# Attention and mixture block on one core: six of eight head groups go through Wo by seven products of halved operands

## The chip, the core and the metric

The kernel runs on one core of a Trainium2 chip. TensorE (PE) multiplies matrices and writes to PSUM; VectorE (DVE), ScalarE (ACT) and GpSimd (POOL) work on tiles of 128 partitions; SyncE (SP) issues all transfers between the chip's memory (HBM) and the tiles in SBUF. The metric is device time in microseconds (us), shown as the median of several runs. Before the change it is 1365.17 us (three runs, 1364.51 to 1367.77).

## The reference

Two batch rows b of 512 tokens with 512 features, all in float32. What matters of the computation:

```python
x  = hidden                                     # (2, 512, 512)
a  = layernorm(x)
q, k, v = a @ Wq + bq, a @ Wk + bk, a @ Wv + bv # inner width 32 heads * 128
q, k = rms_norm(q, gq), rms_norm(k, gk)
p  = softmax(q @ k.T / sqrt(128))               # for each head and batch row
o  = p @ v                                      # (2, 512, 32 * 128)
x  = x + layernorm(o @ Wo + bo)                 # Wo is 4096 x 512
x  = x + layernorm(ffn(layernorm(x)))           # a base product and 8 gated experts of rank 16
```

The change concerns `o @ Wo + bo`.

## The kernel before

The program is one list of instructions whose order on PE, DVE, ACT and POOL is the order in which the code is written (`manual_schedule`, with these four in `IN_ORDER`). Only the place of SP's transfers among each other is left to the scheduler. An instruction that waits holds up all that stand behind it on its engine.

The work comes in stages. First x is loaded and normalized. Then `project` makes Q and afterwards K, group by group of four heads (`GH` = 4, eight groups), each group with seven products of halved operands (tokens of the two batch rows, halves of the features, halves of the group's columns) instead of eight. The finished heads go out to HBM (`keptq`, `keptk`). During Q's groups `value_sums` loads quarters of Wv, forms sums on POOL and stores them (`keptw`). During K's groups the q tiles are fetched back, scaled on DVE and stored (`keptqs`). V is made by `values`, a generator whose every step is one product tile of 512 columns on PE (two matmuls) and an exit from PSUM; finished V tiles go to HBM (`keptv`).

The head loop (`for i in range(N)`, lines 533 to 557) has 64 iterations, `i = 2 * head + batch row`. In iteration i the engines get, in this order: `sums(i - 1)` and `below_top(i)` on DVE (L459 and L467, L484), `scores(i + 1)` on PE with its four exits on ACT (L440, L441), the exponential of i on ACT (L487), `reciprocals` and `divided` for i - 1 (PE L473 writes psd, DVE L475, L477, L502, ACT L503), V steps if any are due, one tile of `outward`, `top_of(i + 1)` (DVE L450, L451, POOL L453), the exits of V and outward on DVE, and last `weighted(i)` on PE (L496), which needs the exponential of i. So PE's order within an iteration is scores, psd, V, outward, weighted. The first 28 V steps run ahead of the loop; 28 more are spread over i = 0 to 7 and the last 56 over i = 8 to 43 (the line that computes `want`).

`outward(g, n)` (L514) multiplies the four heads of group g, 128 tokens of one batch row, by four blocks of Wo into one PSUM tile, and adds it to one of eight tiles `ys` (L515). Group g is done during the eight iterations of group g + 1; the last group comes behind the loop.

A float32 matmul of 512 columns shows in the trace as two records, each with its own load of weights (PEld). PSUM tiles come from two tags, `ps` and `aux`, of four banks each; V, outward and weighted share `aux`. A pool has a fixed number of tiles, and a new one waits until one is free: `opool` holds finished heads, `hpool` the weights of V (three tiles of 512 KB), `wpool` the weights of Q and K and then Wo by groups (two of 1 MB), `vpool` the sums of weights and then V tiles, `kpool` and `qpool` the k and q tiles of the loop. `fetch(i + 3)` and `fetch_v` issue the loop's loads.

Of the kernel before, what the change touches and what calls it, by code (L numbers as in the profile page):

```python
# [10 lines left out]
F32 = mybir.dt.float32  # L11
AF = mybir.ActivationFunctionType
ALU = mybir.AluOpType
AX = mybir.AxisListType

P = 128
S = 512
D = 512
H = 32
INNER = H * P  # L20
NT = S // P
NK = D // P
GH = 4
E, R = 8, 16
# [7 lines left out]
def kernel(ctx: ExitStack, tc: tile.TileContext, x, wq, wk, wv, wo, vecs, rows, wbase, gates, bexp, out):  # L32
# [7 lines left out]

    nc = tc.nc
    B = x.shape[0]
    N = H * B

    const = ctx.enter_context(tc.tile_pool(name="const", bufs=1))
    xpool = ctx.enter_context(tc.tile_pool(name="xpool", bufs=B * NT))
    npool = ctx.enter_context(tc.tile_pool(name="npool", bufs=B * NK))
    ypool = ctx.enter_context(tc.tile_pool(name="ypool", bufs=B * NT))  # L50
    upool = ctx.enter_context(tc.tile_pool(name="upool", bufs=7))
    vpool = ctx.enter_context(tc.tile_pool(name="vpool", bufs=3 * NT))
    qpool = ctx.enter_context(tc.tile_pool(name="qpool", bufs=5))
    kpool = ctx.enter_context(tc.tile_pool(name="kpool", bufs=5))
    opool = ctx.enter_context(tc.tile_pool(name="opool", bufs=GH * B + 5))
    spool = ctx.enter_context(tc.tile_pool(name="spool", bufs=3))
    tmp = ctx.enter_context(tc.tile_pool(name="tmp", bufs=4))
    wpool = ctx.enter_context(tc.tile_pool(name="wpool", bufs=2))
    hpool = ctx.enter_context(tc.tile_pool(name="hpool", bufs=3))
    small = ctx.enter_context(tc.tile_pool(name="small", bufs=4))  # L60
    psum = ctx.enter_context(tc.tile_pool(name="psum", bufs=4, space=bass.MemoryType.PSUM))
    dram = ctx.enter_context(tc.tile_pool(name="dram", bufs=1, space=bass.MemoryType.DRAM))
# [12 lines left out]
            turn_of[0] += 1  # L75
        return psum.tile([P, 512], F32, tag=tag, name=name)

    def load_x(b, t, name):
        xt = xpool.tile([P, D], F32, tag="x", name=f"{name}{b}_{t}")
        nc.sync.dma_start(out=xt, in_=x[b, ts(t, P), :])  # L80
        return xt

    def load_w(src, name):

# [1 line left out]
        nc.sync.dma_start(out=w, in_=src.rearrange("(c p) f -> p c f", p=P))  # L86
        return w

    xs = [[load_x(b, t, "x") for t in range(NT)] for b in range(B)]
    wq0 = load_w(wq[:, ts(0, GH * P)], "w_q0")  # L90

    ident = const.tile([P, P], F32, tag="ident", name="ident")
# [57 lines left out]
    def token_sums(xTs):  # L150

        (b11, b21), (b12, b22) = ((xT[0:2], xT[2:4]) for xT in xTs)
        t1, t2, t3, t4 = (
            [xpool.tile([P, 512], F32, tag="x", name=f"t{i + 1}_{c}") for c in range(2)] for i in range(4)
        )
        for c in range(2):
            nc.vector.tensor_tensor(t1[c], b12[c], b11[c], ALU.subtract)
            nc.vector.tensor_tensor(t2[c], b22[c], t1[c], ALU.subtract)  # L158
            nc.vector.tensor_tensor(t3[c], b22[c], b12[c], ALU.subtract)
            nc.vector.tensor_tensor(t4[c], b21[c], t2[c], ALU.subtract)  # L160
        return [t1, t2, t3, t4]

    def weight_sums(w, name):

        a11, a12, a21, a22 = w[:, 0:2, 0:256], w[:, 2:4, 0:256], w[:, 0:2, 256:512], w[:, 2:4, 256:512]
        out = [vpool.tile([P, 2, 256], F32, tag="v", name=f"s{i + 1}_{name}") for i in range(4)]
        s1, s2, s3, s4 = out
        nc.gpsimd.tensor_tensor(s1, a21, a22, ALU.add)
        nc.gpsimd.tensor_tensor(s2, s1, a11, ALU.subtract)
        nc.gpsimd.tensor_tensor(s3, a11, a21, ALU.subtract)  # L170
        nc.gpsimd.tensor_tensor(s4, a12, s2, ALU.subtract)
        return [a11, a12, a22] + out
# [88 lines left out]
    def attention():  # L261
# [13 lines left out]
        G = GH * B  # L275
# [11 lines left out]
        def value_sums(p, c):  # L287
# [10 lines left out]
            for i, w in enumerate((s1, s2, s3, s4)):  # L298
                nc.sync.dma_start(out=keptw[p, i, c], in_=w)

        keptqs = dram.tile([B, H, P, 512], F32, tag="qs", name="keptqs")

        scale_steps = []
# [28 lines left out]
        for g in project(xTs, sums4, wq, bq, steps[:, 0, :], "q", [(qpool, "q")], keptq, accq, weight_sums(wq0, "q0")):  # L332
            if g == NG - 2:
                k_parts = weight_sums(load_w(wk[:, ts(0, GH * P)], "w_k0"), "k0")
            value_sums(g // 2, g % 2)
        for g in project(xTs, sums4, wk, bk, steps[:, 1, :], "k", [(kpool, "k"), (upool, "u")], keptk, acck, k_parts, between=scale_some):
            if g == 0:
                for b in range(B):
                    ssq = pt(f"ssq{b}")
                    nc.tensor.matmul(ssq, ones, accq[b], start=True, stop=True)  # L340
                    nc.scalar.activation(rqs[b], ssq, AF.Sqrt, bias=epst[:, 1:2], scale=1.0 / INNER)
                    nc.vector.reciprocal(rqs[b], rqs[b])
                scale_steps.extend(scalings())
# [8 lines left out]
        vs, wos = {}, {}  # L352

        def load_wo(g):
            wos[g] = load_w(wo[ts(g, GH * P), :], f"wo{g}")

        keptv = dram.tile([B, H // GH, NT, P, 512], F32, tag="v", name="keptv")

# [54 lines left out]

                    yield exits

        def fetch_v(b, g):
            for t in range(NT):
                v = vpool.tile([P, 512], F32, tag="v", name=f"v{b}_{g}_{t}")
                nc.sync.dma_start(out=v, in_=keptv[b, g, t])
                vs[b, g, t] = v  # L420

        qs, kk = {}, {}

# [62 lines left out]
        def exponentials(i):  # L486
            nc.scalar.activation(ss[i], ss[i], AF.Exp)  # L487

        os = {}

        def weighted(i):
            h, b = divmod(i, B)
            g, j = divmod(h, GH)
            po = pt(f"o{b}_{h}", "aux")
            for k in range(NT):
                nc.tensor.matmul(po, vs[b, g, k][:, ts(j, P)], ss[i][:, k, :], start=(k == 0), stop=(k == NT - 1))  # L496
            return po

        def divided(i, po, r):
            h, b = divmod(i, B)  # L500
            o = opool.tile([P, 512], F32, tag="o", name=f"oh{b}_{h}")
            nc.vector.tensor_tensor(o, po, r, ALU.mult)  # L502
            nc.scalar.activation(o, o, AF.Identity, bias=bv[:, h : h + 1], scale=1.0)  # L503
            os[b, h] = o

        ys = [ypool.tile([P, 512], F32, tag="y", name=f"y{n}") for n in range(B * NT)]

        def outward(g, n, tag=None):

            b, t = divmod(n, NT)  # L510
            ps = pt(f"psy{b}_{g}_{t}", tag or "aux")
            for j in range(GH):
                o = os[b, g * GH + j]
                nc.tensor.matmul(ps, o[:, ts(t, P)], wos[g][:, j, :], start=(j == 0), stop=(j == GH - 1))  # L514
            return lambda: nc.vector.tensor_tensor(ys[n], ps, bo_b if g == 0 else ys[n], ALU.add)  # L515


        v_steps = values()
        for n in range(28):
# [6 lines left out]
            if n == 18:  # L526
                scores(0)
                top_of(0)
        for b in range(B):
            fetch_v(b, 0)  # L530
        left = 28 * (NG // 2 - 1)
        po = None
        for i in range(N):
            g, n = divmod(i, G)
            if i + 3 < N:
                fetch(i + 3)
            if n == 2:
                load_wo(g)
            if n >= G - 2 and g + 1 < NG:
                fetch_v(n - G + 2, g + 1)  # L540
            part = sums(i - 1) if i > 0 else None
            below_top(i)
            if i + 1 < N:
                scores(i + 1)
            exponentials(i)
            if i > 0:
                divided(i - 1, po, reciprocals(i - 1, part))
            exits = []
            want = 28 * (i + 1) // G if i < G else 28 + 56 * (i + 1 - G) // (5 * G - 4)
            while left and 84 - left < want:  # L550
                exits.append(next(v_steps))
                left -= 1
            adds = [outward(g - 1, n)] if g > 0 else []
            top_of(i + 1)
            for work in exits + adds:
                work()
            po = weighted(i)
        divided(N - 1, po, reciprocals(N - 1, sums(N - 1)))
        again = [[kpool.tile([P, 512], F32, tag="k", name=f"xr{b}_{t}") for t in range(NT)] for b in range(B)]
        for b in range(B):  # L560
            for t in range(NT):
                nc.sync.dma_start(out=again[b][t], in_=x[b, ts(t, P), :])
        wb = load_w(wbase, "wb")
        bexp_sb = hpool.tile([P, 2, 512], F32, tag="h", name="bexp_sb")[:, 0, :]
        gate_sb = hpool.tile([P, 1024], F32, tag="h", name="gate_sb")[:, 0 : NK * (E * R + E + 1)].rearrange(
            "p (c f) -> p c f", c=NK
        )
        nc.sync.dma_start(out=gate_sb, in_=gates.rearrange("(c p) f -> p c f", p=P))
        nc.sync.dma_start(out=bexp_sb, in_=bexp)
        adds = [outward(NG - 1, n, "ps") for n in range(NT)]  # L570
        for add in adds:
            add()
        adds = [outward(NG - 1, NT + n, "aux") for n in range(NT)]
        for b in range(B):
            x2 = ys[b * NT : (b + 1) * NT]
            for _ in residual(again[b], x2, f"r{b}"):
                pass
            if b == 0:
# [31 lines left out]
    def ffn(b, xs, w, gate_sb, bexp_sb):  # L610
# [63 lines left out]
        zs = []  # L674
        for t in range(NT):
            nc.tensor.matmul(pss[t], hT[:, ts(t, P)], bexp_sb, start=False, stop=True)  # L676
            z = vpool.tile([P, 512], F32, tag="v", name=f"z{b}_{t}")
            nc.vector.tensor_tensor(z, pss[t], bbase_b, ALU.add)
            zs.append(z)
        yield  # L680
# [41 lines left out]
```

## Time and profile before

| | |
|---|---|
| median of three runs | 1365.17 us |
| the profiled execution | 1363.96 us, of which the span is 1362.2 |
| instructions | 10840 |
| Q stage, about 20 to 225 us | TensorE without idle time from 68 us on |
| K stage, about 225 to 418 us | DMA 312 to 337 GB/s from 272 us on |
| first V steps, 418 to 459 us, then the head loop to about 1265 us | TensorE full but for 3.26 us |
| last group through Wo, norms, mixture, 1265 to 1362 us | TensorE partly idle |
| scores, weighted and Wo on TensorE | 230.2, 230.3 and 230.8 us |
| V on TensorE | 208.3 us |
| traffic | HBM read 136.42 MB, written 77.59 MB |

How to read the profile: all times are in us from the span's start unless marked ns. Busy time counts an engine's instructions, not its waits. A row of the groups gives line, engine, operation, output and inputs, shape and count, then busy time in all and the mean of one in ns, then the engine's idle time ahead of these instructions and what ended it. A row of the timeline gives start, duration and the same names, and in brackets the wait ahead of it. The chain follows back from the last instruction what released each step. Rows of windows give each engine's busy time within a stretch, the granted TensorE clock, the DMA engines' busy share and GB/s. The span of matmuls overlaps with the next one's, so the distance between starts is what one costs in a stream.

### The profile page before, as it was taken

What the parts mean: (1) busy time and instruction counts of PE and PEld (TensorE: products, weight loads), DVE (VectorE), ACT (ScalarE), POOL (GpSimd) and SP (SyncE); (2) the same over time, 40 slices, a digit from 0 to 9 for tenths busy, and PEclk for the clock granted to TensorE, in tenths of its full rate; (3) what the DMA queues carried; (4) which work ended last, traced back from release to release, by engine and by line L of the source; (5) the groups of instructions that cost most, each with busy time, mean ns of one, the idle gap of its engine ahead of it and who ended that gap; (6) DMA issues with size and microseconds to landing.
All of it is one profiled execution on the core that took longest, in us unless ns stands there. A gap on an engine that the chain in (4) does not pass through costs nothing.

```text
span 1362.2 us, 10840 instructions
## 1 busy us (share of the span) xinstructions
PE 1319.9 (97%) x3244; PEld 599.4 (44%) x3244; DVE 926.2 (68%) x1206; ACT 488.0 (36%) x655; POOL 400.9 (29%) x294
## 2 busy tenths in 40 slices
PE   4999999999999999999999999999999999999976
PEld 2444444444444444444444444444444444444443
DVE  6443434777754478877777777777677888888566
ACT  4123232222131153443434334343433455444333
POOL 3478888565763011111111111111111111111000
PEclk9999999999998999999999999999999999999988
DMA  6486665599999865532343252352343131300101
GB/s 218 170 282 220 219 221 201 178 314 337 320 323 311 262 208 161 177 132 85 123 155 103 91 188 62 99 171 91 108 147 101 62 123 55 116 31 24 55 0 62
DMA packets 115083, 214.75 MB, mean 158 GB/s; under 512 B 10192, under 2 KB 10832, under 8 KB 115024
## 3 DMA queue, kind: packets, MB, share of 16 engines
q1 hardware_dynamic: 115024, 214.05, 47.0%
q8 instruction: 26, 0.43, 0.1%
q14 instruction: 33, 0.27, 0.1%
HBM read 136.42 MB, written 77.59 MB: 157 GB/s over the span
## 4 chain that ended last, share of the span: by engine, by line
PE 68%; DVE 2%; DMA 1%; ACT 0%; issue 0%; ACTq 0%
PE pss L440 16%; PE o L496 16%; PE psy L514 16%; PE v L384 14%; PE f L626 2%; PE p_k L192 2%; PE f L676 1%; PE psd L473 1%; PE hg L618 1%; DMA w_v<-keptw 1%; PE nt_f L139 0%; DVE st_z L123 0%; DVE quarters L459 0%; DVE s L484 0%; DVE z L600 0%; ACT s L487 0%
## 5 line engine op out<-in xcount | busy, mean ns | idle before, releaser
L441 ACT ACTIVATE s<-pss,rk 128x512 f32<-128x512 f32 x256 | 175.9, 687 | 464.6 <-PE pss L440 457.8
L453 POOL PARTITION_ALL_REDUCE top<-m x64 | 114.1, 1783 | 717.1 <-DVE m L451 717.1
L514 PE MATMUL psy<-wo,oh 128*128 128x512 f32 x512 | 230.8, 596 | 0.0
L496 PE MATMUL o<-s,v 128*128 128x512 f32 x512 | 230.3, 592 | 0.3 <-ACT s L487 0.3
L440 PE MATMUL pss<-qh,kh 128*128 128x512 f32 x512 | 230.2, 592 | 0.0
L496 PEld LDWEIGHTS o<-s,v 128*128 128x128 f32 x512 | 97.2, 190 | 123.1 <-issue 121.5
L440 PEld LDWEIGHTS pss<-qh,kh 128*128 128x128 f32 x512 | 97.3, 190 | 122.5 <-issue 122.5
L459 DVE TRANSPOSE_TENSOR_REDUCE quarters<-s 128x64 f32<-128x2048 f32 x64 | 147.3, 2301 | 0.0
L484 DVE TENSOR_TENSOR s<-s,top 128x2048 f32<-128x2048 f32 x64 | 146.0, 2281 | 0.0
L514 PEld LDWEIGHTS psy<-wo,oh 128*128 128x128 f32 x512 | 95.7, 190 | 112.4 <-issue 111.9
L487 ACT ACTIVATE s<-s 128x2048 f32<-128x2048 f32 x64 | 121.7, 1901 | 6.1 <-DVE s L484 6.1
L384 PE MATMUL v<-w_v,t 128*128 128x512 f32 x256 | 120.0, 613 | 3.3 <-DMA w_v<-keptw 3.3
L213 POOL TENSOR_TENSOR accq<-accq,sq_q 128x512 f32<-128x512 f32 x62 | 78.6, 1268 | 55.6 <-ACT sq_q L212 54.5
L213 POOL TENSOR_TENSOR acck<-acck,sq_k 128x512 f32<-128x512 f32 x62 | 85.4, 1382 | 24.7 <-ACT sq_k L212 21.7
L192 PE MATMUL p_q<-t,s_q 128*128 128x512 f32 x192 | 87.8, 607 | 2.6 <-DVE t L158 2.6
L384 PE MATMUL v<-w_v,nT_a 128*128 128x512 f32 x192 | 88.3, 601 | 0.0
L212 ACT ACTIVATE sq_k<-k 128x512 f32<-128x512 f32 x62 | 38.7, 630 | 137.8 <-DVE k L244 67.8
L212 ACT ACTIVATE sq_q<-q 128x512 f32<-128x512 f32 x62 | 39.1, 631 | 133.8 <-DVE q L244 78.2
L192 PE MATMUL p_k<-t,s_k 128*128 128x512 f32 x192 | 85.0, 592 | 0.0
L475 DVE RECIPROCAL inv<-psd 128x16 f32<-128x16 f32 x64 | 16.5, 257 | 99.6 <-PE psd L473 99.6
L450 DVE TENSOR_TENSOR m<-s 128x1024 f32<-128x1024 f32 x64 | 77.8, 1216 | 4.7 <-ACT s L441 4.7
L515 DVE TENSOR_TENSOR y<-psy,y 128x512 f32<-128x512 f32 x56 | 38.4, 691 | 57.6 <-PE psy L514 57.6
(152 smaller groups left out, 1418.5 us busy)
## 6 DMA issues: line engine op xcount, KB each, us to landing
keptq<-q SPq DMA_DIRECT2D x64, 256.0 KB, 4.0
q<-keptq SPq DMA_DIRECT2D x16, 1024.0 KB, 6.5
w_v<-keptw SPq DMA_DIRECT2D x32, 512.0 KB, 4.0
keptk<-k SPq DMA_DIRECT2D x64, 256.0 KB, 6.9
keptqs<-q SPq DMA_DIRECT2D x64, 256.0 KB, 6.9
qh<-keptqs SPq DMA_DIRECT2D x64, 256.0 KB, 2.9
kh<-keptk SPq DMA_DIRECT2D x64, 256.0 KB, 2.7
keptv<-o_v SPq DMA_DIRECT2D x64, 256.0 KB, 3.4
```

What stands on the lines that cost most here:

```text
L192: nc.tensor.matmul(ps, a[:, c, ts(j, P)], x[c], start=(c == 0), stop=(c == 1))
L212: nc.scalar.activation(sq, o, AF.Square)
L213: nc.gpsimd.tensor_tensor(accs[b], accs[b], sq, ALU.add)
L384: nc.tensor.matmul(ps, x[c][:, ts(t, P)], w[:, c, :], start=(c == 0), stop=(c == 1))
L440: nc.tensor.matmul(ps, kk[i][:, ts(k, P)], qs[i], start=True, stop=True)
L441: nc.scalar.activation(s[:, k, :], ps, AF.Copy, scale=rks[b][:, k : k + 1])
L453: nc.gpsimd.partition_all_reduce(ms[i], m[:, 0, :], P, ReduceOp.max)
L459: nc.vector.tensor_reduce(quarters.rearrange("p k j -> p (k j)"), ss[i].rearrange("p k (j r) -> p (k j) r", r=32), AX.X, ALU.add, apply_tr ...
L484: nc.vector.tensor_tensor(s, s, top.unsqueeze(1).to_broadcast([P, NT, 512]), ALU.subtract)
L487: nc.scalar.activation(ss[i], ss[i], AF.Exp)
L496: nc.tensor.matmul(po, vs[b, g, k][:, ts(j, P)], ss[i][:, k, :], start=(k == 0), stop=(k == NT - 1))
L514: nc.tensor.matmul(ps, o[:, ts(t, P)], wos[g][:, j, :], start=(j == 0), stop=(j == GH - 1))
```

## The change

For the first six of eight groups (`WG`), o @ Wo is computed by seven products in place of eight. The left operand is halved by batch row and by head within a pair of heads (2c and 2c + 1): a11, a12 are the pair's heads of row 0, a21, a22 those of row 1. The right operand is halved by head within the pair (k) and by columns of Wo (e, 256 each). Two pairs of a group are summed in PSUM.

- During Q's groups Wo's halves are loaded for these six groups (512 KB each, two for each group), four sums are formed in place on DVE (`output_sums`), and stored to HBM (`keptwo`).
- `head_sums(c)`, four DVE operations in every fourth iteration, forms the left sums of a pair.
- `through_wo(g, i, u)` is one task: product i, half u of the tokens, four logical matmuls of 256 columns into one PSUM tile. A group has 14 tasks, laid over the eight iterations of the next group. `load_right` fetches the right operand in rows of 1 KB, into two tiles of a new pool.
- The result is added to one of 14 running sums in SBUF, `acc[i][u]`; for the first group it is written by ACT, or by DVE together with a bias (products 1 and 5). Eight of the 14 lie in the two tiles of `wpool`, where Wo lay before.
- During the last group's iterations `combined` makes the eight y tiles from the running sums, 14 DVE operations, three an iteration. There group 6 goes through Wo as before, with each addition one iteration later; group 7 follows behind the loop as before. Their Wo blocks are now loaded in two halves, from `hpool`.
- V is fetched by pairs of heads, 512 KB in rows of 1 KB, one pair ahead, into four tiles; before it was fetched by groups in four transfers of 256 KB.
- Pools are reshaped to make room (x, weight sums and running sums in larger tiles, `opool` 16 instead of 13, z from `opool`, gates and expert weights from the new pool).

```diff
-    xpool = ctx.enter_context(tc.tile_pool(name="xpool", bufs=B * NT))
+    xpool = ctx.enter_context(tc.tile_pool(name="xpool", bufs=B * NT // 2))
-    ypool = ctx.enter_context(tc.tile_pool(name="ypool", bufs=B * NT))
+    ypool = ctx.enter_context(tc.tile_pool(name="ypool", bufs=6))
-    vpool = ctx.enter_context(tc.tile_pool(name="vpool", bufs=3 * NT))
+    vpool = ctx.enter_context(tc.tile_pool(name="vpool", bufs=4))
-    opool = ctx.enter_context(tc.tile_pool(name="opool", bufs=GH * B + 5))
+    opool = ctx.enter_context(tc.tile_pool(name="opool", bufs=16))
+    gpool = ctx.enter_context(tc.tile_pool(name="gpool", bufs=2))
...
+        def load_halves(g):
+            pool, tag = ((hpool, "h"), (gpool, "g"))[g % 2]
+            wo_halves[g] = [pool.tile([P, 2, 512], F32, tag=tag, name=f"wo{g}_{k}") for k in range(2)]
+            for k in range(2):
+                nc.sync.dma_start(out=wo_halves[g][k], in_=woq[g, k])
+        def output_sums(g):
+            of = wo_halves[g]
+            (b11, b12), (b21, b22) = ([w[:, :, ts(e, 256)] for e in range(2)] for w in of)
+            nc.vector.tensor_tensor(b11, b12, b11, ALU.subtract)
+            nc.vector.tensor_tensor(b12, b22, b12, ALU.subtract)
+            nc.vector.tensor_tensor(b22, b22, b11, ALU.subtract)
+            nc.vector.tensor_tensor(b21, b22, b21, ALU.subtract)
+            for k in range(2):
+                nc.sync.dma_start(out=keptwo[g, k], in_=of[k])
...
             value_sums(g // 2, g % 2)
+            if 0 < g <= WG:
+                output_sums(g - 1)
+            if g < WG:
+                load_halves(g)
...
-        def fetch_v(b, g):
-            for t in range(NT):
-                v = vpool.tile([P, 512], F32, tag="v", name=f"v{b}_{g}_{t}")
-                nc.sync.dma_start(out=v, in_=keptv[b, g, t])
-                vs[b, g, t] = v
+        def fetch_v(b, c):
+            v = vpool.tile([P, NT, 256], F32, tag="v", name=f"v{b}_{c}")
+            src = keptv[b, c // 2].rearrange("t p f -> p t f")
+            nc.sync.dma_start(out=v, in_=src[:, :, ts(c % 2, 256)])
+            vs[b, c] = v
...
+        def head_sums(c):
...
+            a11, a12, a21, a22 = (os[b, 2 * c + k] for b in range(B) for k in range(2))
+            s3, s2, s4 = tile_of(3), tile_of(2), tile_of(4)
+            nc.vector.tensor_tensor(s3, a11, a21, ALU.subtract)
+            nc.vector.tensor_tensor(a21, a21, a22, ALU.add)
+            nc.vector.tensor_tensor(s2, a21, a11, ALU.subtract)
+            nc.vector.tensor_tensor(s4, a12, s2, ALU.subtract)
+            left_of.update({(3, c): s4, (5, c): a21, (6, c): s2, (7, c): s3})
+        product_order = (1, 2, 4, 5, 7, 6, 3)
...
+        def through_wo(g, i, u):
+            ps = pt(f"psw{i}_{g}_{u}", "aux").rearrange("p (t e) -> p t e", t=2)
+            for t in range(2):
+                for j in range(2):
+                    a = left_of[i, 2 * g + j][:, ts(2 * u + t, P)]
+                    nc.tensor.matmul(ps[:, t, :], a, right_of[i, g][:, j, :], start=(j == 0), stop=(j == 1))
+            to = acc[i][u]
+            def add():
+                if g > 0:
+                    nc.vector.tensor_tensor(to, ps, to, ALU.add)
+                elif i in bias_of:
+                    nc.vector.tensor_tensor(to, ps, bias_of[i].unsqueeze(1).to_broadcast([P, 2, 256]), ALU.add)
+                else:
+                    nc.scalar.copy(to, ps)
+            return add
...
+        wo_tasks = {i: [] for i in range(N)}
+        for g in range(WG):
+            for k in range(14):
+                wo_tasks[G * (g + 1) + k * G // 14].append(
+                    lambda g=g, k=k: through_wo(g, product_order[k // 2], k % 2)
+                )
...
-            if n == 2:
-                load_wo(g)
-            if n >= G - 2 and g + 1 < NG:
-                fetch_v(n - G + 2, g + 1)
+            c, n4 = divmod(i, 2 * B)
+            if 2 <= n4 and 0 < c < H // 2 - 1:
+                fetch_v(n4 - 2, c + 1)
+            if g >= WG and n == 6:
+                load_wo(g)
+            if g < WG and n == 7:
+                for k in range(2):
+                    load_right(g, k)
+            if 0 < g <= WG and n in (2, 4):
+                load_right(g - 1, 1 + n // 2)
+            if n == 0 and g > WG:
+                combining = [step for u in range(2) for step in combined(u)]
...
-            adds = [outward(g - 1, n)] if g > 0 else []
+            adds = [task() for task in wo_tasks[i]]
             top_of(i + 1)
+            if n4 == 0 and 0 < c <= 2 * WG:
+                head_sums(c - 1)
+            for _ in range(3):
+                if combining:
+                    combining.pop(0)()
+            if i >= last:
+                held, adds = adds, held
             for work in exits + adds:
                 work()
             po = weighted(i)
+        for add in held:
+            add()
```

In the changed kernel the matmuls of `through_wo` stand in line 580, the additions in 585, the head sums in 557 to 560.

## The prediction

> **What bounds the kernel now.** I read the busy table first, then the chain that ended last, then the groups, and last the timeline of one iteration.
>
> ```profile
> PE 1319.9 (97%) x3244; PEld 599.4 (44%) x3244; DVE 926.2 (68%) x1206; ACT 488.0 (36%) x655; POOL 400.9 (29%) x294
> ...
> PE 68%; DVE 2%; DMA 1%; ACT 0%; issue 0%; ACTq 0%
> ...
> L514 PE MATMUL psy<-wo,oh 128*128 128x512 f32 x512 | 230.8, 596 | 0.0
> ```
>
> TensorE is busy 97% of the span, and in the part that the chain follows back (from 394 us) the chain is TensorE nearly throughout. The product with Wo (L514) takes 230.8 us with no idle time before it. So TensorE work taken from the head loop should shorten the kernel, unless a shorter stretch uncovers something. What could be uncovered is read from one iteration without V products:
>
> ```profile
> 1134.53 0.29 PE L473 MATMUL psd<-part,same 128*128 128x16 f32 x2
> ...
> 1134.85 0.26 DVE L475 RECIPROCAL inv<-psd 128x16 f32<-128x16 f32 x1 [1.59 <-PE psd L473]
> ...
> 1135.31 1.90 ACT L487 ACTIVATE s<-s 128x2048 f32<-128x2048 f32 x1
> ...
> 1138.18 3.60 PE L496 MATMUL o<-s,v 128*128 128x512 f32 x8
> 1138.38 0.69 DVE L515 TENSOR_TENSOR y<-psy,y 128x512 f32<-128x512 f32 x1
> ...
> 1141.50 2.28 DVE L484 TENSOR_TENSOR s<-s,top 128x2048 f32<-128x2048 f32 x1
> ...
> 1145.05 0.29 PE L473 MATMUL psd<-part,same 128*128 128x16 f32 x2
> ```
>
> An iteration is 10.52 us from psd to psd. Three slacks come out of it. VectorE: from its reciprocal to the end of L484 it works 8.93 us without a gap, then waits 1.59 us for psd. The exponential: it ends at 1137.21, and L496, which needs it, starts at 1138.18, so 0.97 us late is free. L484 ends at 1143.78; the next exponential comes at 1145.84, so 2.05 us late is free there.
>
> **TensorE's part.** Before, a group of four heads sends 32 products of 512 columns through Wo, 64 records. After, 14 tasks of 4 products of 256 columns: 112 records for each of six groups. Their price is bounded by the narrowest steady stream in the trace:
>
> ```profile
> 1265.42 27.56 PE psy L514 x64
> ...
> 1328.91 3.76 PE hg L618 x32
> 1332.67 13.73 PE f L626 x32
> ```
>
> The second and third run at a granted clock of 1.00: 137 columns cost 3.76/32 = 117.5 ns, 512 columns 13.73/32 = 429.1 ns, so a column costs 0.831 ns. At 256 columns that gives 117.5 + 119 x 0.831 = 216.4 ns. A group costs 112 x 0.2164 = 24.24 us instead of 64 x 0.4291 = 27.46: 3.22 saved, **19.3 us in six groups**. In strict proportion to columns it would be 20.6. Against it speaks the Trainium skill, "TensorE: Matmul & The Clock Gate", section "Back-to-back issue gap": the spacing of matmuls is set by weight load and matmul together, and a short matmul does not hide its load (its figures: 81 ns sustained at 128 columns, 55.6 isolated, some 25 ns more). Charged to each of the 672 short records this would be 17 us, and the change would save 2 to 4 us of TensorE time. The row decides: 137 columns, shorter still and each with its own load of weights, run at 117.5 ns, 2.8 above their share of 429.1. I take 19.3.
>
> **What the shorter iterations uncover.** The 14 tasks of a group are laid over eight iterations as 2, 2, 2, 1, 2, 2, 2, 1. A task is 8 x 0.2164 = 1.73 us. V products run until i = 43, one or two in every iteration, 1.76 us each, so up to there even a one-task iteration has 3.49 us between psd and L496, as now. At i = 47, 51, 55 there is 1.73 alone. The exponential ends 2.68 us after psd starts, plus 0.06 to be seen; TensorE is ready at 0.13 + 1.73 = 1.86. That is 0.88 three times: **+2.6**.
>
> Sums of heads: four 128x512 tensor_tensors on VectorE in one iteration of four (i = 4 to 48). In the timeline an operation that doesn't need the one ahead starts 0.61 us after it (1138.38, the reduce at 1138.99); one that does starts 0.03 after its end, so 0.72: 0.61 + 2 x 0.72 + 0.69 = 2.75 together. With V products the iteration is 1.76 to 3.5 us longer and VectorE gains 0.61 to 1.2, so they fit. At i = 44 and 48, without V, VectorE has 2.75 and a second addition of 0.61 more, and TensorE's iteration is 10.45 instead of 10.52: 3.43 against 2.05 + 0.97 of slack, some 0.5 each: **+1.1**. It catches up over the next iterations with 0.8 us of slack in each.
>
> PSUM: the tag of V, Wo and L496 has 4 banks. With two V products and two tasks, L496 is the fifth tile of an iteration and takes the first V tile's bank, freed on VectorE behind the head sums. That addition starts at psd + 3.85 + 2.65 and ends at 7.2 (7.8 where the product has two exits); L496 is due at 7.12. Five iterations (16, 20, 24, 36, 40), 0.2 to 0.8: **+1.5**.
>
> The 14 combining additions stand in the first five iterations of the last group, three each: with an addition VectorE then works 10.9 us against 10.52 in three of them and is late by at most 1.2, inside the slacks: 0, with 1 to 2 us if the slack is gone. The ten ScalarE copies of the first group (0.58 each) come behind the exponential on an engine busy 36%: 0.
>
> **The start of V.** Here a stall goes.
>
> ```profile
> 417.82 2.08 SPq L86 DMA_DIRECT2D wo<-in_wo  x1
> ...
> 425.81 0.41 SPq L370 DMA_DIRECT2D w_v<-keptw  x1
> ...
> 433.69 11.75 PE L384 MATMUL v<-w_v,t 128*128 128x512 f32 x20 [3.26 <-DMA w_v<-keptw]
> ```
>
> That w_v took 7.74 us against a median of 4.0, behind two Wo loads of 1 MB that land in 10.0. After, Wo's first loads stand at the end of the Q projection, and only K's and q's transfers are ahead. But four kh fetches now precede w_v on SP's queue, not two (0.5 each), so I put its issue at 425.8 to 426.9. With the 4.7 that these loads take in the median there, it lands at 430.5 to 431.6; TensorE is ready at 430.43. At most 1.2 of 3.26 stays: **-2**; from 0 (other traffic fills the place) to -3.3.
>
> **The Q projection.** 6.3 MB of Wo are read, summed on VectorE (24 operations, four behind each group, some 2.8 us on an engine with 20 of 34 us idle) and 6.3 MB written. On SP the stores wait for these sums with keptq stores behind them.
>
> ```profile
> 170.00:204.00 34.00, 34.00 (x80) 15.01 (x79) 13.57 (x20) 10.37 (x17) 27.84 (x23) 1.00 0.64 222
> 272.00:306.00 34.00, 34.00 (x81) 15.06 (x80) 26.52 (x33) 10.38 (x17) 22.30 (x16) 1.00 0.92 314
> ```
>
> The first row is the Q stage, the second K's: 314 GB/s with TensorE without idle time. A Q group (24 us) moves 5 MB and would move 7: 305 GB/s. So the K stage is the cover: 0, up to +5 if stores come late enough to hold the q tiles. V fetches and right halves in the loop come in rows of 1 KB; the loop's DMA share is 0.1 to 0.56 and each is issued more than an iteration ahead: 0, up to +3 where SP stands at a wait for a buffer with a kh behind it. The last half of wo7 is issued when group 6 leaves TensorE: 3.9 us (the 512 KB w_v load from HBM) against 3.43 + 0.13 + 1.72 of cover: 0. The reshaped buffers (x, weight sums, z, gates) add no instruction, and a weight sum still waits for the same load as before: 0.
>
> **Sum**, against the profiled execution's 1363.96 (span 1362.2 and 1.8 around it): -19.3 + 2.6 + 1.1 + 1.5 - 2.0 = -16.1, so 1347.9. The median shown is 1.2 above that execution, which gives **1349**. Differences below 0.3% (4 us) can't be told from none.
>
> **Rivals.**
> - *All cover holds*: no stalls but the short fills, the whole 3.3 at V's start back, 20.6 on TensorE: 1365.2 - 20.6 - 3.3 + 2.6 = 1344, and 1341 without the fills. Against it: VectorE has 113 more instructions. Chance 0.12.
> - *Half is given back*: SP's order (loads that wait for Wo buffers among kh and keptv) or the fuller DMA of the Q stage costs 5 to 8 us more: 1354 to 1358. For it: SP waits 432 us in total for TensorE before kh fetches, so whatever is ordered behind one is late. Chance 0.19.
> - *Half-width products don't come at half the price* (the rule above): 17 us back, 1365, no change. Against it, the hg row. Chance 0.04.
> - *VectorE sets the pace*: without V products a group of two head sums is 8 x 8.93 + 6 x 0.61 + 2 x 2.75 = 80.6 us on VectorE and 8 x 6.99 + 24.2 = 80.1 on TensorE, already level. If VectorE has no slack where V products run either (its V exits wait for buffers that stores hold, and everything behind them on the engine waits too), each of the ten head sums there (27.5 us) and the 17 further additions (63 tasks for 36, less ten copies on ScalarE; 10.4) is exposed: 1349 + 38 = 1387. It makes the kernel slower once over 20 of these 38 us show. For it: VectorE is busy 28.7 of 34 us in the stretch without V. Against: some 25 of 34 with V. Chance 0.05.
>
> The forecast itself (1344 to 1354) has 0.60. The range 1342 to 1358 leaves out the last two rivals and the ends of the first two. Faster 0.91, same 0.04, slower 0.05.
>
> **What would show it.** L580 in place of L514 at about 146 us for 672 records, 216 ns apart; L514 down to 128 records; idle time before L496 put to the exponential in three iterations of group 5; the w_v wait at V's start near 1 us; the Q stage at 280 to 310 GB/s with TensorE still full. Idle time before L496 or psd in iterations with V products, or kh waits on TensorE, would make the forecast wrong.

## The result, and the profile after

The changed kernel takes **1356.17 us** (median of 8 runs, 1352.07 to 1361.83), the kernel before 1365.36 beside it (8 runs, 1362.99 to 1367.77): a ratio of 0.9934, interval 0.9914 to 0.9954. That is 9 us gained (6 to 12 by the interval) where 16 were forecast.

First the same three lines of the page as were shown of before: the busy table, the chain by engine, and the group that took the place of L496 (line, engine, operation, operands, shape, count, busy time, mean ns of one, then the idle time ahead of it and what ended most of it).

```profile
PE 1302.7 (96%) x3532; PEld 652.7 (48%) x3532; DVE 1032.7 (76%) x1319; ACT 494.8 (37%) x665; POOL 415.0 (31%) x294
...
PE 88%; DVE 9%; ACT 1%; issue 1%; DMA 0%; POOL 0%; ACTq 0%; DVEq 0%; POOLq 0%
...
L530 PE MATMUL o<-s,v 128*128 128x512 f32 x512 | 231.5, 595 | 7.2 <-ACT s L521 3.0
```

TensorE has lost 17 us of busy time, VectorE has gained 107, and the chain, which can now be followed over the whole span, runs through VectorE for 9% of it. The weighted product, which waited 0.3 us in all before, waits 7.2. Next the waits of TensorE within the head loop, from the view of waits of the changed kernel (engine, tile and line, releaser: us in total, times, longest).

```profile
PE o L530 <- ACT s L521: 3.0, 8, 0.6
...
PE psd L507 <- DVE part L501: 1.7, 4, 0.6
...
PE o L530 <- DVE u_v L443: 1.5, 1, 1.5
...
PE o L530 <- DVE u_v L438: 0.9, 1, 0.9
PE o L530 <- DVE u_v L435: 0.9, 1, 0.9
PE o L530 <- issue: 0.8, 1, 0.8
```

The last four rows are the bank waits of i = 16, 20, 24 and 40 (4.1 us in all), the second is the head sums without V and the combining, and the first contains the three short iterations. The brackets count idle time from the modelled end of the last matmul; measured by starts each wait is some 0.2 us longer, since records that follow one another overlap by that much.

To see where the time went, the span is cut at three starts of TensorE: K's first product, V's first product and the first scores; the head loop reaches from these scores to the gate's first product.

| profiled execution of | to K | K stage | V's first pass | head loop | rest | span |
|---|---|---|---|---|---|---|
| before | 223.36 | 194.82 | 40.83 | 837.37 | 65.8 | 1362.2 |
| after | 225.22 | 193.99 | 34.40 | 830.50 | 66.2 | 1350.3 |
| difference | +1.9 | -0.8 | -6.4 | -6.9 | +0.4 | -11.9 |

Both profiles come from executions below the median of their kernel, after's the fastest of its eight, so the 11.9 is more than the 9.2 of the medians. By the forecast the head loop should have lost 14.1 (19.3 less 2.6, 1.1 and 1.5), and it lost 6.9. **These 7.2 us are about the 7 that are missing from the forecast.** What the V stage gave has to be tested too, since one profile may be a chance.

### The profile page after: what moved, and what is told of

Read it like the earlier page. It is cut to its first block, busy times and chain, and to the rows that moved or that the text cites. A ratio compares the mean times of both kernels' runs of the same rounds, so it can differ in the third digit from the quotient of the medians.

```text
span 1350.3 us, 11614 instructions
## 1 busy us (share of the span) xinstructions
PE 1302.7 (96%) x3532; PEld 652.7 (48%) x3532; DVE 1032.7 (76%) x1319; ACT 494.8 (37%) x665; POOL 415.0 (31%) x294
## 4 chain that ended last, share of the span: by engine, by line
PE 88%; DVE 9%; ACT 1%; issue 1%; DMA 0%; POOL 0%; ACTq 0%; DVEq 0%; POOLq 0%
PE v L417 15%; PE p_q L194 15%; PE pss L474 14%; PE o L530 14%; PE p_k L194 14%; PE psw L580 9%; PE psy L622 2%; PE f L763 2%; DVE quarters L493 1%; DVE s L518 1%; ACT s L521 1%; PE f L813 1%; DVE m L484 1%; PE hg L755 1%; DVE y L612 1%
## 5 line engine op out<-in xcount | busy, mean ns | idle before, releaser
L487 POOL PARTITION_ALL_REDUCE top<-m x64 | 119.1, 1861 | 700.4 <-DVE m L485 700.4
L530 PE MATMUL o<-s,v 128*128 128x512 f32 x512 | 231.5, 595 | 7.2 <-ACT s L521 3.0
L530 PEld LDWEIGHTS o<-s,v 128*128 128x128 f32 x512 | 96.1, 190 | 114.0 <-issue 102.5
L417 PE MATMUL v<-w_v,t 128*128 128x512 f32 x256 | 116.8, 600 | 0.0
L580 PE MATMUL psw<-wr,oh 128*128 128x256 f32 x384 | 88.3, 380 | 0.0
L580 PEld LDWEIGHTS psw<-wr,oh 128*128 128x128 f32 x384 | 72.5, 190 | 19.8 <-issue 11.5
L347 DVE SCALAR_TENSOR_TENSOR q<-q,gqk,rq 128x512 f32<-128x512 f32 x64 | 72.6, 1175 | 0.0
```

The source lines that it names most:

```text
L417: nc.tensor.matmul(ps, x[c][:, ts(t, P)], w[:, c, :], start=(c == 0), stop=(c == 1))
L487: nc.gpsimd.partition_all_reduce(ms[i], m[:, 0, :], P, ReduceOp.max)
L530: nc.tensor.matmul(po, vs[b, c][:, k, ts(j, P)], ss[i][:, k, :], start=(k == 0), stop=(k == NT - 1))
L580: nc.tensor.matmul(ps[:, t, :], a, right_of[i, g][:, j, :], start=(j == 0), stop=(j == 1))
```

## The experiments

Times are medians with the ratio to the kernel before on the same chip; the head loop is read from the profile, as above. The loop of before is the same within 0.01 us in three profiles, that of after within 0.03 in three, while the stages before it vary by several us. So the loop decides between theories about the loop.

| kernel | time, us | ratio, interval | K stage | V's first pass | head loop |
|---|---|---|---|---|---|
| before, again | 1367.19 (one run) | | 198.77 | 36.18 | 837.38 |
| b4, before without V's wait | 1361.29 | 0.9974, 0.9963 to 0.9985 | 193.99 | 35.22 | 837.37 |
| c1, after as it is | 1353.59 | 0.9918, 0.9904 to 0.9933 | 196.91 | 34.40 | 830.48 |
| e5, without the sums of Wo | 1352.71 | 0.9913, 0.9896 to 0.9930 | 193.99 | 34.40 | 830.47 |
| e1, sums behind the exits | 1345.94 | 0.9862, 0.9843 to 0.9880 | 195.37 | 34.40 | 824.14 |
| e2, sums an iteration later | 1348.80 | 0.9880, 0.9859 to 0.9901 | 200.38 | 34.63 | 822.89 |
| d1, maximum behind the sums | 1351.15 | 0.9904, 0.9887 to 0.9921 | 194.86 | 34.64 | 825.85 |
| e3, sums and combining moved | 1343.07 | 0.9853, 0.9834 to 0.9872 | 199.44 | 34.41 | 820.26 |
| f2, e3 and the exponential ahead | 1339.80 | 0.9815, 0.9791 to 0.9839 | 197.19 | 35.66 | 818.21 |

### The kernel after as it is (c1)

> The changed kernel as it is, on the same chip as the next three: 1352 to 1362 us as in its eight runs. If its spread (10 us there, 5 us for the kernel before) comes from the chip and not from the kernel, the kernel before should spread as much here.

The loop is the one of the first profile within 0.02 us, and all waits in it are the same. The time on this chip is 1353.59, 11.4 us under the kernel before there, where the first chip gave 9.2; the intervals overlap. Its six runs spread over 3.5 us and the eleven of the kernel before over 7.0, so the 10 us of the first eight runs are not a property of the changed kernel alone. The next three kernels are held against this one.

### Head sums behind the exits (e1)

```diff
             top_of(i + 1)
-            if n4 == 0 and 0 < c <= 2 * WG:
-                head_sums(c - 1)
...
             for work in exits + adds:
                 work()
+            if n4 == 0 and 0 < c <= 2 * WG:
+                head_sums(c - 1)
             po = weighted(i)
```

> The head sums stand behind the exits of V and Wo instead of ahead of them; nothing else is changed. Theory A (TensorE's waits at i = 16, 20, 24, 40 are for the first V tile's PSUM bank, held by head sums that GpSimd's reduction stretches from 0.69 to 1.34 us): the four waits (4.1 us, and 0.24 behind each for a product that starts from rest) go, the stretched operation is back near 0.7 us, and the time falls by 4 to 6 us. Rival B (VectorE has too much to do in these iterations, wherever it stands): the waits move to the exponential or to psd, and the time falls by less than 2 us. The waits at i = 44 and 48 should stay or grow, since there nothing but VectorE's amount of work is at fault.

7.65 us less time than c1 and 6.3 less in the loop, more than the 4 to 6 expected: the four bank waits are gone, and, against the expectation, so are the waits of psd for i = 44 and 48, so these were no matter of VectorE's amount of work alone. The second of the four sums takes 0.69 us here, as expected. The theory that the sums, standing ahead of V's exits on VectorE, hold the PSUM bank is upheld. But the edit moves the sums away from GpSimd's all-reduce as well, so it doesn't tell the place from the longer sum.

### Head sums one iteration later (e2)

```diff
             below_top(i)
+            if n4 == 1 and 0 < c <= 2 * WG:
+                head_sums(c - 1)
             if i + 1 < N:
                 scores(i + 1)
```

> The head sums stand one iteration later, behind the subtraction of the top and ahead of the reciprocal, where VectorE waited 1.6 us for psd. Theory A: as the first, and the waits at i = 44 and 48 (0.77 each with psd's) go too, since the sums fill idle time: 6 to 8 us less than the control. Rival B: no better than the first.

Here the time misled: 4.8 us less than c1, short of the forecast and slower than e1. The loop is the shortest of the three, 7.6 below c1. In the profiled execution, one of the slower of its six, what hid it lies in the K stage, which this edit doesn't touch. The timeline of e2 there:

```profile
341.73 6.00 SPq L348 DMA_DIRECT2D keptqs<-q  x5
...
345.33 1.41 DVE L347 SCALAR_TENSOR_TENSOR q<-q,gqk,rq 128x512 f32<-128x512 f32 x2 [3.63 <-DMA q<-keptq]
...
349.79 0.99 PE L194 MATMUL p_k<-nT_a,w_k 128*128 128x512 f32 x1 [1.96 <-DVE q L347]
```

VectorE waits 3.63 us for a q tile on its way back from HBM, K's exits are queued behind it, and TensorE waits 1.96 us for VectorE in its turn (by the order of the code, for a PSUM bank that such an exit frees). The DMA engines move 305 GB/s from 330 to 340 us and 385 from 340 to 350. Such waits come and go in both kernels: the K stage takes 194.0 us without one and up to 200.4 with two. With the slower clock behind some of them they make the differences between the K stages of the table, and so part of the spread of the times; that they make all of it in the runs without a profile is not shown.

### Without the sums of Wo (e5)

This one leaves out the loads, sums and stores of Wo in the Q stage and takes all right operands from Wo itself, so what it computes differs in that part.

```diff
-            if 0 < g <= WG:
-                output_sums(g - 1)
-            if g < WG:
-                load_halves(g)
...
-                src = (woq if i <= 3 else keptwo)[g, k]
+                src = woq[g, k]
```

> Wo's halves are not loaded, summed and stored during the Q projection; all seven products read the plain blocks of Wo, so the output is not the reference's. 12.6 MB less traffic and 24 VectorE operations less in the Q stage. Theory A (the Q stage hides them, as the profiled run shows): the median within 1.5 us of the control, and the same spread. Rival C (they cost time in the runs that were not profiled, whose median is 4 us above the profiled one): 3 to 5 us less than the control in the median, and a narrower spread.

0.9 us less, within the intervals, with the same loop and no narrower spread (6.4 us). The added 12.6 MB cost nothing that can be measured. Two rows of the windows of the kernel after show why (stretch, length, busy time and count of PE, PEld, DVE, ACT and POOL, granted clock, DMA share, GB/s):

```profile
102.00:136.00 34.00, 34.00 (x81) 15.05 (x80) 22.50 (x27) 9.57 (x15) 29.53 (x23) 1.00 0.95 345
...
170.00:204.00 34.00, 34.00 (x81) 15.06 (x80) 21.83 (x27) 10.41 (x17) 28.64 (x23) 1.00 0.92 319
```

The second stands at 0.92 and 319 GB/s where the kernel before stood at 0.64 and 222, and TensorE still has no gap.

### V's first pass in the kernel before (before again, b4)

> The kernel before as it is, for a second trace of it. Theory (the start of V costs the kernel before 3.3 us of waiting and then some 3 us of a lower clock, every time): the 76 V records from V's first product to the first scores take 41 us again, with a wait of 3 to 3.5 us for a tile of w_v and a granted clock below 0.95 in the 15 us behind it. Rival (a chance of that one profile): 34.5 to 37 us. The head loop, from the first scores to the gate's first product, is 837.4 us within 0.5 in both.

```diff
+            early = [opool.tile([P, 512], F32, tag="o", name=f"w7_early{c}") for c in range(2)]
+            for c in range(2):
+                nc.sync.dma_start(out=early[c], in_=keptw[0, 2, c])
...
-                if n + 2 < len(todo):
-                    ws.append(weights(todo[n + 2][0], todo[n + 2][2]))
+                if n == 1:
+                    ws.append(early)
+                for m in ({0: (2,), 1: (4,), 2: ()}.get(n, (n + 2,))):
+                    if m < len(todo):
+                        ws.append(weights(todo[m][0], todo[m][2]))
```

> The kernel before, with the weights of V's fourth product loaded ahead of the stage into two tiles that stand free there, so that nothing of V's first pass waits for a transfer; nothing else is changed. Theory (what V's start gave was 3.3 us of waiting and as much again through the clock that the wait took away): V's first pass takes 34.5 us as in the kernel after, the clock stays at 1.00 through it, and the time falls by 5 to 7 us against before. Rival 1 (the wait alone counts): 3 to 3.5 us. Rival 2 (the transfers are merely moved and some other tile is late): under 1 us.

The theory of 41 us each time falls. Three rows of windows, the first two from the first profile of before, the third from the second, each behind its wait for w_v:

```profile
426.00:434.00 8.00, 4.74 (x18) 2.50 (x17) 2.25 (x4) 0.26 (x1) 0.00 (x0) 0.92 1.04 383
434.00:442.00 8.00, 8.00 (x13) 3.29 (x13) 1.38 (x2) 0.00 (x0) 0.00 (x0) 0.65 0.74 241
```

```profile
434.00:442.00 8.00, 6.45 (x21) 3.09 (x20) 2.25 (x4) 0.26 (x1) 0.00 (x0) 1.00 0.98 363
```

The first profile waited 3.26 us, and over the next 8 us the granted clock was 0.65: 13 records where 20 are usual. The second waited 1.55 at an unbroken clock, and its pass took 36.18. With the weights there early (b4) the time falls by 2.9 us of the medians, by the interval 2.0 to 5.0: nearest to rival 1, with the theory's 5 at the very end of the interval, and a wait of 0.58 for VectorE still stood in its profile. So of the 6.4 us between the profiles before and after some 3 are the usual worth of V's start, by estimate, and the rest belongs to that one execution.

### The maximum behind the sums (d1)

e1 and e2 say that moving the sums helps, not why their old place costs so much more than forecast. The iteration i = 16 in the timeline of the kernel after shows one thing out of line:

```profile
685.21 0.69 DVE L485 TENSOR_TENSOR m<-m 128x512 f32<-128x512 f32 x1
...
685.82 0.69 DVE L557 TENSOR_TENSOR s_o<-oh,oh 128x512 f32<-128x512 f32 x1
...
686.07 2.08 POOL L487 PARTITION_ALL_REDUCE top<-m  x1 [10.47 <-DVE m L485]
686.61 1.34 DVE L558 TENSOR_TENSOR oh<-oh,oh 128x512 f32<-128x512 f32 x1
687.98 0.69 DVE L559 TENSOR_TENSOR s_o<-oh,oh 128x512 f32<-128x512 f32 x1
688.70 0.69 DVE L560 TENSOR_TENSOR s_o<-oh,s_o 128x512 f32<-128x512 f32 x1
689.31 1.28 DVE L425 TENSOR_TENSOR o_v<-v,u_v 128x512 f32<-128x512 f32 x2
...
690.10 3.67 PE L530 MATMUL o<-s,v 128*128 128x512 f32 x8 [0.84 <-issue]
```

Four sums of one shape, and the second takes 1.34 us where the others take 0.69: in all 12 places, while GpSimd's all-reduce runs. L530 takes the bank that the first of the two exits in L425 frees. All twelve of the second sum, here and, in the second row, in d1 (count, shortest, median and longest in ns, first and last start, shape):

```profile
L558 DVE TENSOR_TENSOR oh<-oh,oh x12: 1339/1340/1342, 532.7 to 1092.9; 128x512 f32<-128x512 f32 x12
```

```profile
L561 DVE TENSOR_TENSOR oh<-oh,oh x12: 691/692/693, 532.8 to 1089.1; 128x512 f32<-128x512 f32 x12
```

d1 leaves VectorE the same instructions ahead of the exits and only lets the second maximum, for which GpSimd waits, stand behind the sums:

```diff
             nc.vector.tensor_tensor(m, s[:, 0:2, :], s[:, 2:4, :], ALU.max)
+            if between:
+                between()
             nc.vector.tensor_tensor(m[:, 0, :], m[:, 0, :], m[:, 1, :], ALU.max)
...
-            top_of(i + 1)
-            if n4 == 0 and 0 < c <= 2 * WG:
-                head_sums(c - 1)
+            top_of(i + 1, (lambda: head_sums(c - 1)) if n4 == 0 and 0 < c <= 2 * WG else None)
```

> The kernel after, with the four head sums moved by one VectorE instruction, between the two maxima of the next head's top, so that they run ahead of GpSimd's all-reduce and not beside it; VectorE has the same instructions ahead of the exits as in the kernel after. Theory (half of the longer bank waits comes from the one sum that takes 1.34 in place of 0.69 us beside the all-reduce): L558's instruction at 0.69 in all 12, the waits for VectorE at i=16, 20, 24 and 40 shorter by 0.65 each, those of the head sums' own products at i=44 and 48 gone, the head loop 827 us in place of 830.5, the time 3 to 4 us under that of the kernel after. Rival (only the number of instructions ahead of the exits counts, or the stretched sum just moves to another one): loop within 0.7 of 830.5.

The same iteration in d1 (L561 is the second sum, L488 the second maximum):

```profile
685.86 0.69 DVE L560 TENSOR_TENSOR s_o<-oh,oh 128x512 f32<-128x512 f32 x1
...
686.65 0.69 DVE L561 TENSOR_TENSOR oh<-oh,oh 128x512 f32<-128x512 f32 x1
...
688.71 0.68 DVE L488 TENSOR_TENSOR m<-m 128x512 f32<-128x512 f32 x1
689.32 1.28 DVE L425 TENSOR_TENSOR o_v<-v,u_v 128x512 f32<-128x512 f32 x2
689.57 1.78 POOL L490 PARTITION_ALL_REDUCE top<-m  x1 [13.20 <-DVE m L488]
690.10 2.38 PE L533 MATMUL o<-s,v 128*128 128x512 f32 x5
```

The sum is back at 0.69 in all 12, the all-reduce at 1.78, and the exits that now run beside it (one input from PSUM, one from SBUF) take what they always took. The loop is 825.85, 4.6 below c1: the theory, by a little more than its 3.5, because the waits at i = 16, 20 and 40 fell below what the trace lists, i = 24 kept 0.71 of 1.48, and psd's for i = 44 and 48 went. The time, 1351.15 on another chip, can't carry this alone: its interval and c1's overlap.

### The combining moved as well (e3)

```diff
             below_top(i)
             if n4 == 1 and 0 < c <= 2 * WG:
                 head_sums(c - 1)
+            for _ in range(3 if n < 2 else 2):
+                if combining:
+                    combining.pop(0)()
...
-            for _ in range(3):
-                if combining:
-                    combining.pop(0)()
```

This is e2's kernel with that edit.

> The kernel after with both pieces of VectorE work in slack places: head sums one iteration later behind the subtraction of the top, and the combining steps behind that subtraction too, by 3, 3, 2, 2, 2, 2 of them. Theory (all that came back in the head loop came from such work ahead of exits and of the next sums): the waits of 0.21 to 0.34 us before the sums' and the weighted products at i=56 and 57 go, with their restarts; head loop 821 to 822 us in place of 822.9 with the head sums moved alone; time 8 to 10 us under that of the kernel after, less whatever the K stage's waits for its transfers add. Rival (combining there only makes other waits): loop 823 or more.

820.26, which is 2.6 below e2 and a little under the 821 to 822 of the theory. Five of the fourteen combining sums had met the all-reduce in the kernel after. The timeline of one such iteration there, with what it made late:

```profile
1198.53 0.69 DVE L612 TENSOR_TENSOR y<-acc_y,acc_y 128x512 f32<-128x512 f32 x1
1198.78 2.08 POOL L487 PARTITION_ALL_REDUCE top<-m  x1 [9.38 <-DVE m L485]
1199.13 1.53 DVE L612 TENSOR_TENSOR y<-acc 128x512 f32<-128x512 f32 x1
...
1204.52 0.37 PE L507 MATMUL psd<-part,same 128*128 128x16 f32 x2 [0.21 <-DVE part L501]
```

1.53 us in place of 0.69, and psd of the next iteration late by 0.21. In e3 all fourteen run in 0.68 to 0.69. The edit changes their place and their number in an iteration together with what GpSimd does beside them, so what each of these is worth is not told apart.

### The exponential ahead in the short iterations (f2)

```diff
             for k in range(NT):
...
                 nc.tensor.matmul(ps, kk[i][:, ts(k, P)], qs[i], start=True, stop=True)
+                if k == NT - 1 and early is not None:
+                    exponentials(early)
...
-                scores(i + 1)
-            exponentials(i)
+                scores(i + 1, i if i in (47, 51, 55) else None)
+            if i not in (47, 51, 55):
+                exponentials(i)
```

> The kernel with head sums and combining moved, and besides, at i = 47, 51 and 55 alone, ScalarE takes the exponential of i ahead of the last of the four exits of the next scores. Theory (the short iterations wait because the exponential stands behind four exits on ScalarE in order; it could start at the end of the subtraction, 0.4 to 0.6 us sooner): the three waits of 0.63 us before the weighted products go, with their restarts, and the head loop falls from 820.3 to 817.5 to 818.5 us; with that nothing is left of what came back but the shorter products, 837.4 less 19.3. Rival (the maximum behind the late exit then holds VectorE, and a wait of the same size comes back in the next iteration): 820 or more. In time both are within 3 us of the kernel with both moves, and the noise of the K stage decides.

818.21, 2.05 below e3. The timeline of i = 51:

```profile
1114.88 0.29 PE L509 MATMUL psd<-part,same 128*128 128x16 f32 x2
...
1115.28 1.91 ACT L523 ACTIVATE s<-s 128x2048 f32<-128x2048 f32 x1 [0.36 <-DVE s L520]
...
1117.24 3.70 PE L532 MATMUL o<-s,v 128*128 128x512 f32 x8 [0.24 <-ACT s L523]
1117.66 0.71 ACT L539 ACTIVATE oh<-oh,vec 128x512 f32<-128x512 f32 x1
1117.80 1.22 DVE L486 TENSOR_TENSOR m<-s 128x1024 f32<-128x1024 f32 x1 [0.85 <-ACT s L477]
```

0.24 us of the 0.63 is left at this one, since the exponential now waits for VectorE's subtraction itself; VectorE's 0.85 for the late exit makes nothing else late. **This is the fastest version**: 1339.80 us against 1365.26 on the same chip, a gain of 25.5 us where the change by itself gave 9.2 and, on another chip, 11.4. Of this 19.2 lie in the loop; the rest comes from V's start and from stages that vary.

## Why the prediction was partly right

The time lay within the range of 1342 to 1358, but outside the forecast's own 1344 to 1354 and 7 us above the 1349. That it stayed inside was in part luck: it fell where the rival that half is given back had been put, for another cause. One of the signs that were to make the forecast wrong is there too: TensorE stands idle before the weighted product in iterations with V products, 4.1 us in all. By its steps:

- **TensorE's part, -19.3: right.** With all that came back taken away (f2) the loop is 837.37 - 818.21 = 19.2 shorter. The chain of the kernel after gives the spacing directly (start, duration, what):

```profile
582.59 3.45 PE psw L580 x16
586.05 3.43 PE o L530 x8
```

  3.45/16 is 215.6 ns for a record of 256 columns, where the row of hg gave 216.4. The rule that a short matmul doesn't hide its load of weights, weighed there, would have left 2 to 4 us; the row was right to decide. (Two small slips: by its own figures that row lies 2.7 ns above its share, not 2.8, and the section cited gives about 56 ns, not 55.6, for the isolated matmul.) The 146 us that the page was to show for L580 are 154.9 there, because the page's busy time counts the overlapping ends of its runs; 672 x 0.2156 is 144.9.
- **The short iterations, +2.6: right.** 0.88 was forecast for each. In the trace they show 0.63 of idle time, and 0.24 more by starts. f2 took 2.05 of it back and left a part.
- **The PSUM bank, +1.5, and the head sums without V, +1.1: the step that failed.** Together 2.6 was forecast; e2, which takes all of both away, gave 7.6. The mechanism and four of the five iterations were right (there was no wait at i = 36); the size was wrong. It rested on four sums taking 2.75 us together, from the durations of such operations in the timeline of before, and they take 3.57 (685.82 to 689.39 in the rows above), 0.65 of it because one of them runs beside GpSimd's all-reduce; in d1 they take 2.93. d1 removes that overlap alone and gives 4.6 in six places; 3.0 is left, close to the 2.6. With the slack used up, the delay counted in full here. (A smaller slip: 3.43 against 2.05 + 0.97 of slack is 0.41 late for each of i = 44 and 48, so 0.8 and not 1.1.)
- **The combining, 0: the other step that failed.** e3 gave 2.6, more than the 1 to 2 that were named for the case without slack. It was costed at 0.61 for each sum, and five of fourteen took 1.41 to 1.53.
- **The start of V, -2.0: right within what can be told.** b4 puts its usual worth at 2.9 (2.0 to 5.0). The wait of about 1 us that was to stay is there in some executions only: 1.02 in f2's profile, none in the other seven of kernels with the changed V stage.
- **The Q stage, SP's order and the late half of wo7, 0: right.** The Q stage moved 265 to 345 GB/s in windows of 34 us, wider than the 280 to 310 forecast, with TensorE full; e5 gave 0.9, within the noise, and no wait of TensorE for kh, v or a right operand stands in the loop of any of these profiles.

With the two terms as measured, 7.6 for 2.6 and 2.6 for nothing, the forecast's sum becomes 1349 + 5.0 + 2.6 = 1356.6, against 1356.17. The closeness is better than the times allow, as c1 shows. The rival that half is given back named 1354 to 1358 but gave SP's order and the fuller DMA as the cause. Its time came true, its mechanism didn't. VectorE didn't set the pace either: the same VectorE work in other places takes 818 us.

What the Trainium skill says, "SBUF — State Buffer", section "Who interferes with whom", bears on the failed step: a VectorE instruction with two inputs from SBUF contends with a GpSimd instruction that reads SBUF, since its second input comes through an interface that both share, and one with a single SBUF input doesn't. The prediction did not weigh it. The rows agree on who contends: sums of two SBUF tiles went from 0.69 to 1.34 or more, exits with an input from PSUM took no longer than before (0.69 or less) beside the same all-reduce. The spans also look like one waiting for the other, the exclusive lock of which the section speaks, more than like two that share: in all 17 places of the kernel after the longer sum ended 0.20 us before the all-reduce did, whether it had started 0.35, 0.47 or 0.54 us behind it, and the all-reduce took 2.08 for 1.78 each time, where a sum had started 0.25 us ahead of it. The runs show that the overlap is the cause; that the read interface is what they wait for rests on the page, and GpSimd's spans are rough.

## What to carry to other kernels

Where work is added to an in-order engine, ask not only whether it fits into the iteration but what stands behind it: here the same instructions cost 7.6 us ahead of exits that free a PSUM bank, and nothing that can be seen one iteration later, away from the all-reduce and from the exits. A duration from a quiet place of the trace holds only where the neighbour is the same; look what GpSimd does beside each new VectorE operation with two inputs from SBUF. And compare the stage that an edit touches in the two profiles, since a noisy stage elsewhere can turn the order of two versions in their times, as it did with e1 and e2.

## What had not been expected of the hardware

- The all-reduce and VectorE's sums slow each other down: 0.69 to 1.34 us in twelve head sums, to 1.41 or 1.53 in five combining sums, and 1.78 to 2.08 on GpSimd.
- TensorE's clock behind a wait doesn't go by the length of the wait. Sixteen records of 512 columns took 8.80, 8.80 and 8.56 us behind waits of 1.96, 2.85 and 3.76 in the K stage, and 7.10 or 7.11 behind others of 2.27, 2.43 and 2.97. After the 3.26 of the first profile of before the clock averaged 0.65 for 8 us, and V's first pass took 6.4 us more than 34.40.
- The traces' records of the granted clock say what does count. In all eleven, the stretches between two changes are whole multiples of 3.413 us (the last, which is cut off, left aside). Cut by that grid, the stretch from 60 to 1290 us has four pieces in which TensorE was idle for 1.96, 2.34, 2.85 and 3.30 us, and the clock fell to half at the end of each of the four; it fell behind no piece with 1.65 or less. The waits of 2.27, 2.43 and 2.97 fell across a boundary, as 1.42 + 0.85, 1.45 + 0.98 and 1.63 + 1.34. So what counted there was how much of a wait lay within one piece, and the boundaries lie elsewhere in each execution. Before 60 us pieces with 1.94 and 2.01 left the clock alone, so no exact limit comes out of this.
